# Group norm's pieces one engine a step, the end's fp8 rounding partly on GpSimd, and a later centring of the second chunk

## The chip, the cores and the metric

The kernel runs on one core of one Trainium2 chip. The metric is device time in microseconds: the median of several executions. A hardware profile of one more execution shows what each engine did. The engines are called PE (TensorE matmul; PEld is its weight load), DVE (VectorE), ACT (ScalarE), POOL (GpSimd) and SP (SyncE, which here only issues DMAs). Each works through its own queue in order; semaphores make one wait for another.

## The reference

The input x is 4 images of 64 x 64 positions with 96 channels, all in fp32. Cut to what matters:

```python
x = x + conv(_gn(x))            # _gn: group norm, 32 groups of 3 channels, over a whole image
t = tokens(x)                   # 4096 tokens of 96 channels per image
t = t + attn(_ln_t(t))          # 6 heads, no softmax: (q k^T) v, so k^T v comes first
t = t + ffn(_ln_t(t))           # 96 -> 384 -> 96, operands rounded to fp8 (e5m2), sums to fp16

# conv: layer norm, a projection to value, gate, delta and to A, B, C (16 states a channel)
h_new = d * (A_t * h) + d * (B_t * u_t)      # over the 4096 positions in turn
y = g_t * sum(C_t * h_new)                   # then a projection back to 96 channels

# ffn
h = relu(q_acc(q_acc(q_mul(x) @ q_mul(W1).T) + q_mul(b1)))
y = q_acc(q_acc(q_mul(h) @ q_mul(W2).T) + q_mul(b2))
```

The attention has no softmax, so its whole effect on an image is one 97 x 96 matrix, made from the Gram matrix of all tokens of the image. An image's attention can only start when its last token has been through the conv.

## The kernel before, in words

**Tiling.** An image is cut into 8 chunks of 512 tokens (NCH); 4 images give N = 32 chunks. The conv's state has 16 x 96 = 1536 rows, 12 tiles of 128 rows (NT). So the body has K = 384 steps: one step is one tile of one chunk, a 128 x 512 scan along time. In step s the loop at L1401 issues B's projection and copy for tile s+3 (L804, L811), A's for s+1 (L819, L823), C's for s (L844), POOL's multiply for s+2 (L814), the scan (L830), C's multiply (L854 on DVE, or L860 on ACT and L863 on POOL), and then `call(s)`, which runs what was put down for that step with `at(step, fn)`. The order of the work is thus written out by hand: the order in which a step issues its instructions is the order of each engine's queue.

**PSUM.** Matmul results go to banks by tag (L95): A 2, B 1, C 1, D 1 and M 3. All that is not a projection of the scan takes the M ring in turn; the fourth user of the ring waits until the first bank was read.

**Around the body.** For each chunk a `Front` (L659) centres and scales with the group norm's result (L670, L673), does the layer norm, splits the result into a high and a low part, and projects it. `tail` (L907) sums the states, projects, adds, normalizes (L396 on ACT, or L403 on DVE), adds to the Gram matrix and writes the transposed tokens to DRAM. `ffn` (L1059) fetches them (L1071), applies the attention matrix (a_ps, L1076), adds (L1081), takes layer-norm statistics on DVE (L371, L373), their root on POOL (L378, L392; with L383 and L384 if ACT is to normalize), normalizes to fp8, transposes (xq_ps, L1091), rounds (xq, L1098), and makes three 128 x 512 pieces of the hidden layer (h_ps, L1102).

**Group norm.** `group_norm` (L629) puts the pieces of images 1 to 3 into steps of the image before. Sums of all chunks are gathered by ACT (L574). Then L654 puts down six pieces: moments in step 1 after the last chunk's sum, mean in step 2, root in 4, diagonal in 6, spread and spread_out in 8. A piece holds instructions of several engines: moments has two on DVE (L581, L582) and three on POOL (L583 to L585); mean has a matmul (L590), two reads on DVE (L592, L594) and two on POOL (L596, L597); root has a matmul (L602), DVE (L604) and POOL (L605).

**Weights.** The weights of attention and ffn are transposed on PE and copied out on DVE in the same step (L334 to L359), one weight every 12 steps from step 20.

**The start and the end** are not in steps. They go through `Plan` (L412): jobs with an engine, a cost, what they follow, and the buffers they take and free. `run` lays them out greedily by cost, tries random changes of rank (`tries`, 800 for the end) and keeps the order with the earliest end by its own costs; the jobs are then issued in that order. Gaps that it expects on PE are filled with matmuls that nobody reads (`awake`, L1434). In the start the second chunk's centring on POOL follows a job `calm` at time 22 (L1257, L1328). There the weights of the projections are split: a high part on ACT (`high`, L301), a low part on DVE or POOL (`low`, L259), then copies by SP (L262, L263).

**The end** is what does not fit into the body: the last three chunks of image 2 and the ffn of all of image 3, whose attention matrix needs the last chunk. For each chunk: ACT copies three hidden pieces to fp16 (h, L1119), DVE adds the bias and takes relu (L1123), ACT rounds all three to fp8 at once (hq, L1127), PE projects (y_ps, L1133), the result is rounded to fp16 (DVE for odd chunks, L1141; ACT for even ones, L1143), and POOL adds bias (L1148) and x (L1155); DVE does it for the last two chunks. In image 3 DVE normalizes the even chunks (`vector`, L1067), ACT the odd ones. Chunks are written (image, chunk), such as (3,7).

Of the kernel before, what the change touches and what calls it, by code (L numbers as in the profile page):

```python
# [9 lines left out]
F32 = mybir.dt.float32  # L10
# [3 lines left out]
AF = mybir.ActivationFunctionType  # L14
# [14 lines left out]
NT = NCG * NSH  # L29
# [34 lines left out]
def conv_attn_hybrid_kernel(  # L64
# [38 lines left out]
    def bank(tag, shape, name):  # L103
        return psum.tile(shape, F32, tag=tag, name=name, bufs=BANKS[tag])
# [229 lines left out]
    def weights_attention():  # L334
        ps = bank("M", [C, CA], "wq_ps")
        nc.tensor.transpose(ps, w_qkv[:, 0:C], ident[:CA, :CA])
        nc.vector.tensor_copy(w_qt[0:C, :], ps)

    def weights_ffn1():
        ps = bank("M", [C, HID], "w1_ps")  # L340
        for m in range(NK):
            nc.tensor.transpose(ps[:, m * P : (m + 1) * P], w1_sb[:, m, :], ident)
        nc.vector.tensor_copy(w1_q, ps, saturate=False)

    def weights_ffn2():
        ps = bank("M", [P, NK, C], "w2_ps")
        for m in range(NK):
            nc.tensor.transpose(ps[:, m, :], w2_sb[:, m * P : (m + 1) * P], ident[:C, :C])
        nc.vector.tensor_copy(w2_q, ps, saturate=False)

    def weights_bias():
        ps = bank("M", [P, NK], "b1_ps")
        nc.tensor.transpose(ps, b1_sb, ident[:NK, :NK])
        b1_8 = small.tile([P, NK], F8, tag="b1_8", name="b1_8", bufs=1)
        nc.vector.tensor_copy(b1_8, ps, saturate=False)
        nc.vector.tensor_copy(b1_q, b1_8)
        b2_8 = small.tile([P, C], F8, tag="b2_8", name="b2_8", bufs=1)
        nc.vector.tensor_copy(b2_8, b2_sb, saturate=False)
        nc.vector.tensor_copy(b2_q, b2_8)  # L359
# [52 lines left out]
    class Plan:  # L412
# [10 lines left out]
        def job(self, engine, cost, fn, *args, after=(), take=(), free=(), late=0.0):  # L423

            j = dict(
                engine=engine, cost=cost, fn=fn, args=args, take=take, free=free, late=late,
                after=[a for a in after if a], tail=None, end=None, rank=self.rank,
            )
            self.jobs.append(j)
            return j  # L430
# [96 lines left out]
    def at(step, fn, *args):  # L527
        steps.setdefault(step, []).append((fn, args))
# [4 lines left out]
    class GroupNorm:  # L533
# [45 lines left out]
        def moments(self):  # L579
            t = small.tile([C, 2], F32, tag="gt", name=f"gt_{self.b}", bufs=2)  # L580
            nc.vector.tensor_reduce(t, self.s, AX.X, ALU.add)  # L581
            nc.vector.tensor_scalar_mul(t, t, 1.0 / L)  # L582
            nc.gpsimd.tensor_tensor(self.mv[:, 0:1], t[:, 0:1], self.c, ALU.subtract)  # L583
            nc.gpsimd.tensor_tensor(t[:, 0:1], t[:, 0:1], t[:, 0:1], ALU.mult)
            nc.gpsimd.tensor_tensor(self.mv[:, 1:2], t[:, 1:2], t[:, 0:1], ALU.subtract)  # L585


        def mean(self):
            ps = bank("M", [C, 2], f"gm_ps_{self.b}")
            nc.tensor.matmul(ps[:, 0:1], lhsT=third, rhs=self.mv[:, 0:1], start=True, stop=True)  # L590
            self.m = small.tile([C, 2], F32, tag="gm", name=f"gm_{self.b}", bufs=2)
            nc.vector.tensor_copy(self.m[:, 0:1], ps[:, 0:1])  # L592
            w = small.tile([C, 1], F32, tag="gw", name=f"gw_{self.b}", bufs=2)
            nc.vector.tensor_tensor(w, self.mv[:, 0:1], ps[:, 0:1], ALU.subtract)  # L594
            engine = nc.gpsimd if self.b else nc.vector
            engine.tensor_tensor(w, w, w, ALU.mult)  # L596
            engine.tensor_tensor(w, w, self.mv[:, 1:2], ALU.add)  # L597
            self.w = w

        def root(self):  # L600
            ps = bank("M", [C, 2], f"gv_ps_{self.b}")
            nc.tensor.matmul(ps[:, 0:1], lhsT=third, rhs=self.w, start=True, stop=True)  # L602
            v = small.tile([C, 1], F32, tag="gv", name=f"gv_{self.b}", bufs=2)
            nc.vector.tensor_scalar(v, ps[:, 0:1], 1e-5, None, ALU.add)  # L604
            nc.gpsimd.tensor_tensor(self.m[:, 1:2], v, mhalf[0:C, 0:1], ALU.pow)  # L605


        def diagonal(self, k0=0, k1=2):
# [20 lines left out]
    def group_norm(b, s0):  # L629
        q = {}  # L630

        def make():
            q["g"] = GroupNorm(b)
            q["g"].first()

        def call(name, *args):
            getattr(q["g"], name)(*args)

        when = [s0 + AT["sums"] + NT * n for n in range(NCH)]
        if b == 1:
            when = [8, 15, 22, 29, 36, 43, 50, 57]
        if b > 1:
            at(when[0] - 7, load_gx, b, 0)
        at(when[0] - 2, make)
        for n in range(NCH):
            if n:
                at(max(when[n] - 7, when[n - 1]), load_gx, b, n)
            at(when[n], call, "sums", n)  # L650
            at(when[n] + AT["sums_out"] - AT["sums"], call, "sums_out", n)
        for n, name in ((1, "moments"), (2, "mean"), (4, "root"), (6, "diagonal"), (8, "spread"),
                        (8, "spread_out")):
            at(when[-1] + n, call, name)  # L654


    split, rep, gate = {}, {}, {}
# [233 lines left out]
        {"ACT": 0.5, "DVE": 2.5, "POOL": 1.5},  # L891
    )
    end.last = {}
    end.tries = 800

    def place(plan, s0):

# [161 lines left out]
    def ffn(b, i, s0):  # L1059
# [4 lines left out]
        def tile_of(tag, drain_tag, shape, dtype, name):  # L1064
            return sb(drain_tag if phase["end"] else tag, shape, dtype, f"{name}_{nm}")

        vector = b == B - 1 and i % 2 == 0  # L1067

        def fetch():
            v["xa"] = next_of(xal_t, "xal")  # L1070
# [53 lines left out]

        def quant():
            v["hq"] = sb("bu", [P, NK, TC], F8, f"hq_{nm}")
            nc.scalar.activation(v["hq"], v["h16"], AF.Copy, saturate=False)  # L1127

        def project_out():
            ps = v["ps"] = bank("A" if phase["end"] else "M", [P, J, C], f"y2_ps_{nm}")  # L1130
# [6 lines left out]

        def round_out():
            v["y16"] = tile_of("y16", "xs", [P, J, C], F16, "y16")
            if phase["end"] and i % 2:  # L1140
                nc.vector.tensor_copy(v["y16"], v["ps"])  # L1141
            else:
                nc.scalar.copy(v["y16"], v["ps"])  # L1143

        def bias_out():
            last_two = phase["end"] and b == B - 1 and i > NCH - 3
# [23 lines left out]
        )  # L1170
        done = place(plan, s0)
        if fetch not in done and b < B - 1:
            at(K - 4, fetch)
            done.add(fetch)
        if store in done:
            return
# [10 lines left out]
        def job(engine, cost, fn, *args, **kw):  # L1187
            return None if fn in done else end.job(engine, cost, fn, *args, **kw)
# [10 lines left out]
        if hidden not in done:  # L1199
            r, h, c = [], None, None  # L1200
            for m in range(NK):
                h = job("PE", 0.24, hidden, m, after=[a, h], take=[f"M:{m}{nm}"],
                        free=[f"h:{nm}"] if m == 2 else [])
                c = job("ACT", 0.57, round_hidden, m, after=[h, c],
                        take=[f"rep:{nm}"] if m == 0 else [], free=[f"M:{m}{nm}"])
                r.append(job("DVE", 0.5, relu_vector, m, after=[c]))
            a = job("ACT", 1.5, quant, after=r, take=[f"bu:q{nm}"], free=[f"rep:{nm}"])
        a = job("PE", 0.5, project_out, after=[a], take=[f"A:y{nm}"], free=[f"bu:q{nm}"])
        a = job(*(("ACT", 0.48) if vector else ("DVE", 0.56)), round_out, after=[a],
                take=[f"xs:{nm}"], free=[f"A:y{nm}"])  # L1210
        last_two = b == B - 1 and i > NCH - 3
        a = job(*(("DVE", 0.6) if last_two else ("POOL", 0.95)), bias_out, after=[a], take=[f"xl:{nm}"], free=[f"xs:{nm}"])
# [9 lines left out]
    def planned_start():  # L1222
# [20 lines left out]
        b = mm(0.8, bias_turn, after=[b], key="M:b")  # L1243
        b = job("DVE", 0.35, bias_out, after=[b], free=["M:b"])
        a = job("DVE", 0.4, q.aggregate, after=a)
        m = job("DVE", 1.1, q.mean, after=[a])
        r = job("DVE", 0.7, q.root, after=[m], late=0.9)
        g = []
        for n, a in enumerate((m, r)):
            a = job("ACT", 0.37, q.diagonal, n, n + 1, after=[a, *g])  # L1250
# [9 lines left out]
        wd = job("SP", 1.0, split_copies, w_dug[:, 0], w_dug[:, 1], w_dug[:, 2], after=[ld], late=2.2)  # L1260
        wr = [job("ACT", 0.45, repeat, n, k, after=[(hd, ld)[n]]) for n in range(2) for k in range(2)]
        w = {"rep": job("SP", 1.0, split_copies, *(w_rep[:, n] for n in range(3)), after=wr, late=2.2)}
        for sh in range(NSH):
            plan.rank = 3 * sh - 3
            for k in range(3):
                t = job("ACT", 0.83, high, k, sh, after=[raw[k]])
                if sh < 2:
                    t = job("DVE", 0.8, low, k, sh, nc.vector, after=[t])
                else:
                    plan.rank = 1 if k == 0 else 3 * sh - 3  # L1270
                    t = job("POOL", 1.3, low, k, sh, nc.gpsimd, after=[t, calm])
                    low_b = t if k == 0 else low_b
                v = w_bac[k][:, :, :, sh * P : (sh + 1) * P]
                w[k, sh] = job("SP", 1.0, split_copies, *(v[:, n] for n in range(3)), after=[t], late=2.4)
        plan.rank = -4
# [49 lines left out]


        plan.rank = 1
        a = job("POOL", 1.0, second.centre, nc.gpsimd, after=[*g, calm])  # L1328
        a = job("POOL", 1.0, second.scale, nc.gpsimd, after=[a])
        a = job("DVE", 1.1, second.stats, after=[a])  # L1330
        a = job("POOL", 1.8, second.ln.rstd, after=[a])
# [35 lines left out]

    second = planned_start()

    for n, fn in enumerate((weights_attention, weights_ffn1, weights_ffn2, weights_bias)):  # L1370
        at(NT + 8 + NT * n, fn)
    for b in range(B):
        for i in range(NCH):
            g = b * NCH + i
# [96 lines left out]
```

## Time and profile before

| what | us |
|---|---|
| median of 3 executions | 1183.2 |
| their range | 1182.86 to 1183.66 |
| the profiled execution, its own time | 1184.49 |
| its span, first to last instruction | 1182.8 |
| PE busy (of the span) | 1140.1 (96%) |
| PEld busy | 874.6 (74%) |
| DVE busy | 1113.2 (94%) |
| ACT busy | 817.3 (69%) |
| POOL busy | 1030.3 (87%) |
| mean granted PE clock | 0.988 of full |

The shares are means over three stages with different limits: a start of about 60 us, the body, and an end from about 1105 us on. So the stages are to be read apart: busy time by stretch, who waited for whom in a stretch, and the chain that ended last. A row of instructions gives engine, line, operation, output and inputs, shape and count, then the busy time and the mean duration of one. Matmuls overlap, so a full PE row says that PE always had something in flight. The granted clock is the share of the full PE clock that the core was given; fillers such as `awake` count as busy.

### The profile page before, as it was taken

What the parts mean: (1) busy time and instruction counts of PE and PEld (TensorE: products, weight loads), DVE (VectorE), ACT (ScalarE), POOL (GpSimd) and SP (SyncE); (2) the same over time, 40 slices, a digit from 0 to 9 for tenths busy, and PEclk for the clock granted to TensorE, in tenths of its full rate; (3) what the DMA queues carried; (4) which work ended last, traced back from release to release, by engine and by line L of the source; (5) the groups of instructions that cost most, each with busy time, mean ns of one, the idle gap of its engine ahead of it and who ended that gap; (6) DMA issues with size and microseconds to landing.
All of it is one profiled execution on the core that took longest, in us unless ns stands there. A gap on an engine that the chain in (4) does not pass through costs nothing. (4 is left out here: it accounts for less than half of the span.)

```text
span 1182.8 us, 19203 instructions
## 1 busy us (share of the span) xinstructions
PE 1140.1 (96%) x5899; PEld 874.6 (74%) x5899; DVE 1113.2 (94%) x2093; ACT 817.3 (69%) x1826; POOL 1030.3 (87%) x1176
## 2 busy tenths in 40 slices
PE   5999999999999999999999999999999999999885
PEld 4777777677777777777777777777777777777573
DVE  6999999899999999999999999999999999999865
ACT  4666655556556777877877777777776777776476
POOL 5798887788889899999999999999999999988554
PEclk8999999899999999999999999999999999999989
DMA  7676776687776776787777777766777778667221
GB/s 185 142 167 143 167 155 154 141 176 161 170 160 151 161 162 157 158 190 170 161 159 161 172 162 166 171 158 152 159 165 169 160 162 185 147 145 153 60 75 47
DMA packets 104288, 182.12 MB, mean 154 GB/s; under 512 B 42637, under 2 KB 50769, under 8 KB 104186
## 3 DMA queue, kind: packets, MB, share of 16 engines
q1 hardware_dynamic: 90060, 106.96, 37.3%
q0 software_dynamic: 13536, 73.93, 31.4%
q8 instruction: 46, 0.75, 0.3%
q14 instruction: 56, 0.46, 0.1%
q10 hardware_dynamic: 590, 0.02, 0.0%
HBM read 69.12 MB, written 24.77 MB: 79 GB/s over the span
## 5 line engine op out<-in xcount | busy, mean ns | idle before, releaser
L814 POOL TENSOR_TENSOR bu<-bu,rep 128x512 f32<-128x512 f32 x384 | 512.9, 1345 | 43.3 <-ACT state L840 34.8
L830 DVE TENSOR_TENSOR_SCAN h<-Aps,state,bu 128x512 f32<-128x512 f32 x336 | 426.2, 1268 | 0.7 <-POOL ch L863 0.5
L811 ACT ACTIVATE bu<-Bps,b_bac 128x512 f32<-128x512 f32 x384 | 263.1, 685 | 198.5 <-PE Bps L269 192.9
L823 DVE SCALAR_TENSOR_TENSOR Aps<-Aps,b_bac,rep 128x512 f32<-128x512 f32 x384 | 281.9, 734 | 8.2 <-PE Aps L269 8.2
L269 PE MATMUL Bps<-xs,w 128*128 128x512 f32 x768 | 268.0, 430 | 7.7 <-ACT bu L811 7.1
L269 PE MATMUL Aps<-xs,w 128*128 128x512 f32 x768 | 242.2, 396 | 1.2 <-DVE h L830 1.0
L863 POOL TENSOR_TENSOR ch<-ch,h 128x512 f32<-128x512 f32 x126 | 170.4, 1352 | 7.9 <-ACT ch L860 3.7
L269 PEld LDWEIGHTS Aps<-xs,w 128*128 128x128 f32 x768 | 143.9, 188 | 37.3 <-DVE h L830 3.0
L269 PEld LDWEIGHTS Bps<-xs,w 128*128 128x128 f32 x768 | 126.7, 191 | 51.2 <-ACT bu L811 15.4
L269 PE MATMUL Aps<-xl,w 128*128 128x512 f32 x384 | 152.0, 396 | 0.0
L269 PE MATMUL Bps<-xl,w 128*128 128x512 f32 x384 | 151.7, 395 | 0.0
L269 PE MATMUL Dps<-xs,w 128*128 128x512 f32 x384 | 121.0, 396 | 0.0
L269 PE MATMUL Cps<-xs,w 128*128 128x512 f32 x384 | 120.6, 395 | 0.0
L854 DVE SCALAR_TENSOR_TENSOR ch<-Dps,b_bac,h 128x512 f32<-128x512 f32 x160 | 118.6, 742 | 0.9 <-PE Dps L269 0.5
L869 POOL DMA_DIRECT2D ch<-ch x94 | 89.6, 953 | 0.3 <-DMA ch<-ch 0.3
L269 PEld LDWEIGHTS Bps<-xl,w 128*128 128x128 f32 x384 | 72.5, 189 | 17.7
L269 PEld LDWEIGHTS Dps<-xs,w 128*128 128x128 f32 x384 | 72.3, 188 | 17.7
L269 PEld LDWEIGHTS Aps<-xl,w 128*128 128x128 f32 x384 | 72.2, 188 | 17.7
L269 PEld LDWEIGHTS Cps<-xs,w 128*128 128x128 f32 x384 | 72.0, 188 | 17.6
L860 ACT ACTIVATE ch<-Cps,b_bac 128x512 f32<-128x512 f32 x94 | 64.6, 688 | 24.1 <-PE Cps L269 24.1
L269 PE MATMUL Dps<-xl,w 128*128 128x512 f32 x192 | 75.9, 395 | 0.0
L269 PE MATMUL Cps<-xl,w 128*128 128x512 f32 x192 | 75.8, 395 | 0.0
(200 smaller groups left out, 2045.2 us busy)
## 6 DMA issues: line engine op xcount, KB each, us to landing
ch<-ch POOLq DMA_DIRECT2D x94, 768.0 KB, 6.7
rep<-ddd SPq DMA_DIRECT2D x124, 384.0 KB, 7.4
ddd<-dd SPq DMA_DIRECT2D x31, 384.0 KB, 3.2
xl<-lo SPq DMA_DIRECT2D x62, 128.0 KB, 2.5
x<-in_x_dram SPq DMA_DIRECT2D x32, 192.0 KB, 3.0
xatd<-xat SPq DMA_DIRECT2D x32, 192.0 KB, 3.6
xal<-xatd SPq DMA_DIRECT2D x32, 192.0 KB, 2.8
out_dram<-o SPq DMA_DIRECT2D x32, 192.0 KB, 2.1
```

The source lines that it names most:

```text
L269: nc.tensor.matmul(ps, lhsT=wt[:, n], rhs=mv, start=(n == 0), stop=(n == 2))
L811: nc.scalar.activation(self.bu, self.b_ps, AF.Identity, bias=self.bias(0))
L814: nc.gpsimd.tensor_tensor(self.bu, self.bu, rep[self.b, self.i][:, 1, self.cg], ALU.mult)
L823: nc.vector.scalar_tensor_tensor(self.a_ps, self.a_ps, self.bias(1), rep[self.b, self.i][:, 0, self.cg], ALU.add, ALU.mult,)
L830: nc.vector.tensor_tensor_scan(self.h, self.a_ps, self.bu, 0.0 if self.i == 0 else state[self.sh, self.cg], ALU.mult, ALU.add,)
L854: nc.vector.scalar_tensor_tensor(self.slot(), self.c_ps, self.bias(2), self.h, ALU.add, ALU.mult)
L860: nc.scalar.activation(self.ch, self.c_ps, AF.Identity, bias=self.bias(2))
L863: nc.gpsimd.tensor_tensor(self.ch, self.ch, self.h, ALU.mult)
L869: nc.gpsimd.dma_start(chs[g, 0], chs.pop((g, sh)), accum_op=ALU.add)
```

## The change

Four edits, and two that follow them:

- **Group norm.** The six pieces become eleven, each of one engine, one to a step, from the step after the last chunk's sums: moments (DVE), variances (POOL), a matmul, mean (DVE), squares (POOL), a matmul, offset (DVE), root (POOL), diagonal (ACT), spread (PE), spread_out (ACT). In the start the pieces are called together in the old order.
- **Weights.** A weight's copy on DVE is put one step after its transposes on PE.
- **The end.** A chunk whose number is divisible by 3 is rounded to fp8 on ACT, the others on POOL. All of y is rounded to fp16 on ACT. In image 3 only chunks 0 and 4 are normalized by DVE; 2 and 6 go to ACT. The plan's costs follow, relu's cost goes from 0.5 to 0.47, and 1500 orders are tried instead of 800. The order of the chunks changes with it: (2,6) before (2,7), and in image 3 chunk 0 goes from third place to last but one.
- **The start.** The second chunk's centring follows POOL's first low split instead of `calm`.
- **Fetches.** Those of image 2 that are left are put into step K - 1 instead of K - 4.

```diff
     def weights_attention():
         ps = bank("M", [C, CA], "wq_ps")
         nc.tensor.transpose(ps, w_qkv[:, 0:C], ident[:CA, :CA])
-        nc.vector.tensor_copy(w_qt[0:C, :], ps)
+        return lambda: nc.vector.tensor_copy(w_qt[0:C, :], ps)
...
+        def variances(self):
+            t = self.t
             nc.gpsimd.tensor_tensor(self.mv[:, 0:1], t[:, 0:1], self.c, ALU.subtract)
...
+        def group_sums(self, name):
+            self.ps = bank("M", [C, 2], f"g{name}_ps_{self.b}")
+            nc.tensor.matmul(
+                self.ps[:, 0:1], lhsT=third, rhs=self.mv[:, 0:1] if name == "m" else self.w,
+                start=True, stop=True,
+            )
...
-        for n, name in ((1, "moments"), (2, "mean"), (4, "root"), (6, "diagonal"), (8, "spread"),
-                        (8, "spread_out")):
-            at(when[-1] + n, call, name)
+        chain = (
+            ("moments",), ("variances",), ("group_sums", "m"), ("mean",), ("squares",),
+            ("group_sums", "v"), ("offset",), ("root",), ("diagonal",), ("spread",), ("spread_out",),
+        )
+        for n, args in enumerate(chain):
+            at(when[-1] + AT["sums_out"] - AT["sums"] + 1 + n, call, *args)
...
-    end.tries = 800
+    end.tries = 1500
...
-        vector = b == B - 1 and i % 2 == 0
+        vector = b == B - 1 and i % 4 == 0
...
-            nc.scalar.activation(v["hq"], v["h16"], AF.Copy, saturate=False)
+            if i % 3 == 0:
+                nc.scalar.activation(v["hq"], v["h16"], AF.Copy, saturate=False)
+            else:
+                nc.gpsimd.tensor_copy(v["hq"], v["h16"], saturate=False)
...
-            if phase["end"] and i % 2:
-                nc.vector.tensor_copy(v["y16"], v["ps"])
-            else:
-                nc.scalar.copy(v["y16"], v["ps"])
+            nc.scalar.copy(v["y16"], v["ps"])
...
-            at(K - 4, fetch)
+            at(K - 1, fetch)
...
-                r.append(job("DVE", 0.5, relu_vector, m, after=[c]))
-            a = job("ACT", 1.5, quant, after=r, take=[f"bu:q{nm}"], free=[f"rep:{nm}"])
+                r.append(job("DVE", 0.47, relu_vector, m, after=[c]))
+            a = job(*(("ACT", 1.5) if i % 3 == 0 else ("POOL", 1.6)), quant, after=r, take=[f"bu:q{nm}"], free=[f"rep:{nm}"])
...
-        a = job("POOL", 1.0, second.centre, nc.gpsimd, after=[*g, calm])
+        a = job("POOL", 1.0, second.centre, nc.gpsimd, after=[*g, first_low])
...
+    def turned(step, fn):
+        at(step + 1, fn())
+
     for n, fn in enumerate((weights_attention, weights_ffn1, weights_ffn2, weights_bias)):
-        at(NT + 8 + NT * n, fn)
+        at(NT + 8 + NT * n, turned, NT + 8 + NT * n, fn)
```

The lines of the changed kernel lie up to 27 further down: POOL's new rounding is L1152, ACT's L1150, h L1141, relu L1145, and y L1165.

## The prediction

> **What bounds the kernel now.** I read the busy time by stretches first, then the chain that ended last, then each queue of the end. Columns of the stretches: length, then busy time (x instructions) of PE, PEld, DVE, ACT, POOL, then granted clock, DMA share, GB/s.
>
> ```profile
> 600.00:800.00 200.00, 199.35 (x1052) 153.84 (x1051) 194.49 (x364) 153.84 (x354) 188.28 (x218) 1.00 0.73 164
> 1109.20:1142.00 32.80, 31.06 (x202) 22.67 (x201) 21.44 (x94) 18.50 (x34) 15.37 (x26) 0.84 0.25 74
> 1142.00:1174.10 32.10, 23.52 (x198) 16.08 (x195) 21.39 (x75) 30.67 (x52) 17.09 (x24) 1.00 0.18 50
> ```
>
> In the body PE and DVE are both full; POOL has 6% left and ACT a quarter. From 1142 to 1174 ACT is the bound (30.67 of 32.10) while POOL is half idle. Before 1142 no engine but PE is full, and PE runs part of it at half clock:
>
> ```profile
> 1126.00:1128.00 2.00, 2.00 (x13) 2.00 (x13) 0.81 (x2) 1.68 (x2) 0.10 (x1) 0.59 0.36 98
> 1132.00:1134.00 2.00, 2.00 (x12) 2.00 (x11) 1.51 (x4) 2.00 (x6) 1.82 (x4) 0.50 0.03 8
> 1136.00:1138.00 2.00, 2.00 (x15) 1.34 (x14) 0.04 (x1) 0.59 (x1) 0.86 (x1) 0.85 0.73 201
> ```
>
> The chain that ended last says the same of the last 35 us: start, length, engine and line.
>
> ```profile
> 1168.54 2.40 ACT h L1119 x5
> 1170.94 2.76 ACT hq L1127 x2
> 1173.71 0.05 issue
> 1173.75 0.70 PE y_ps L1133 x12
> 1174.45 0.02 issue
> 1174.48 0.57 DVE y L1141
> 1175.05 0.02 issue
> 1175.07 0.57 DVE yb L1148
> 1175.64 0.02 issue
> 1175.66 1.15 DVE o L1155
> ```
>
> So the pace of the end is ACT's: copies (0.48 each), quantizations (1.38), then a tail of 5.9 us. DVE ends at 1176.8; 6.0 us follow to the end of the span, and 1.7 lie around it (1184.5 against 1182.8).
>
> **Part 1, group norm and weight copies in pieces.** Nothing is added or removed; per image eleven pieces stand one to a step, so no engine meets in one step a piece it must wait for. In the chain of the three later images DVE waits for none of its small reads. What waits is POOL: L583 for DVE's sums 4.0 us in 3 times, L605 1.1 us in two (of 6.7, 5.6 is the start's). POOL's idle time costs nothing while the scans are fed, and DVE's scans stand end to end there (728.43, 731.50, 734.25, 736.79). PE's sequencer waits before the first sum, half a microsecond in each of three images:
>
> ```profile
> L590 PEldq EVENT_SEMAPHORE  x4: 51/503/649, 12.2 to 726.4; - x4
> ```
>
> Bounds: a gain of 3 x 0.6 = 1.8 if PE's wait is all on the path; a loss where an "M" bank (three in all) is now held a step longer. That is so ten times (four weights, six sums). Only behind the biases is the third user of the ring so close that it must wait: L931's transposes began at 193.24, and the delayed copy would free the bank near 193.7, a loss of 0.5. As PE shows 0.65 us idle in 200, I take a third of the gain, -0.6, and keep -1.8 and +0.5.
>
> **Part 2, the start.** POOL's first low split (1.16: the two at 23.18 take 2.31) goes before centre and scale (1.03 and 1.08). All end where they ended, at 25.5; centring comes 1.16 later, near 24.4. DVE's queue reads it at 30.46 (L371), so 6 us cover it; without that cover it would cost 1.2. SP's copies of that split are issued at 28.1, after others, so nothing is gained. ACT's two copies for the third weight move one or two places forward: one (0.84) falls into ACT's wait of 0.72 before 30.95. Bounds -0.3 to +0.3, by the waits of these rows; I take 0. The later fetches of image 2 (K - 1 instead of K - 4) keep their places in SP's queue and change only which of (2,6) and (2,7) comes first; that is in part 3.
>
> **Part 3, the end.** By engine, from the rows of the end:
>
> - ACT: 7 quantizations leave (chunks 5, 7 of image 2; 1, 2, 4, 5, 7 of image 3), -7 x 1.38 = -9.7; 6 roundings of y come from DVE, +6 x 0.37 = +2.2; chunks 2 and 6 are normalized on ACT, +2 x 1.44 = +2.9. Net -4.6.
> - DVE: -6 x 0.56 - 2 x 1.0 = -5.4.
> - POOL: +2 x 0.6 for two shifts (L383, L384), +7 quantizations.
>
> A quantization on POOL (128x1536, f16 to fp8) isn't in the trace. Nearest rows:
>
> ```profile
> L208 POOL CAST ident<-ident 128x128 fp8e5<-128x128 f32 x1 | 0.3, 291 | 0.1
> L220 POOL MEMSET xn<- 128x512 fp8e5 x2 | 1.1, 528 | 0.1
> L1148 POOL TENSOR_TENSOR yb<-y,b_q 128x384 f16<-128x384 f16 x30 | 27.7, 923 | 7.7 <-ACT y L1143 5.9 <-DVE y L1141 1.6
> ```
>
> Memsets of 1 and 512 columns take 0.10 and 0.53: 0.84 ns a column. At that pace the cast's 0.291 holds 0.18 of fixed cost, and 1536 columns give 0.18 + 1.29 = 1.5; with the 0.19 of a one-column L584 it is 1.4. If the fixed cost were only a memset's 0.10, a column would cost 1.5 ns and the piece 2.4. The two-input row's 2.4 ns a column would need less than no fixed cost, so I drop it. I take 1.5, by the cast row, and keep 1.4 and 2.4.
>
> I then walked the changed queues with these durations. (1) Image 3's attention matrix: a_ps of chunk (2,6) goes first, so the output of (3,7) starts 1.05 earlier; its root comes at 1118.6 instead of 1120.2, and rmat near 1124.2 instead of 1125.4: -1.2. (2) That gain is lost: PE's h_ps of (2,7) is now split by the a_ps of (3,6) and (3,1). At half clock, from 1124.2: two a_ps 3.0, xq 0.4, a filler 0.5, y 1.0, two h 0.8, two a_ps 3.4, the third h 0.5: 1133.8. ACT's copy of it stands ahead of the normalizing of (3,3): copy 0.5, two normalizings 2.9, three small pieces 1.3, and 0.6 for PE between them, so the copies of (3,3) start at 1139.1 (before: 1138.45). (3) From there ACT has 24 copies (11.5), 4 normalizings (5.8), 2 quantizations (2.8), 6 xq (2.9) and 6 y (2.2), 25.1 us, to the last h copy of (3,7), which would end at 1164.2. (4) POOL takes the quantization of (2,7) at 1134.9, as soon as that third copy is through relu. Behind it in its queue stand four roots with shifts (1.97 each), two without (1.4), four more quantizations (1.57 with the gap) and eleven pieces of bias and total (0.97): 29.3 us without a gap, to 1164. ACT waits for them: 1.75 before (3,5)'s normalizing, 1.1 and 0.9 at (3,0) and (3,6), 1.25 in four small ones, 5.0 in all. The last h copy ends near 1169.2 (before 1170.9). (5) The tail: relu 0.3, POOL 1.5, PE 0.75, ACT 0.45, DVE 0.6 and 1.3, and six hops of 0.06: 5.3 (before 5.9). DVE ends near 1174.5 instead of 1176.8: **-2.3**. POOL is late next.
>
> The new POOL pieces meet DVE's:
>
> ```profile
> 1140.35 1.03 DVE L403 TENSOR_SCALAR xn<-x,mv_f,rstd_f 128x96 fp8e5<-128x96 f32 x4
> 1161.93 2.93 DVE L403 TENSOR_SCALAR xn<-x,mv_f,rstd_f 128x96 fp8e5<-128x96 f32 x4
> ```
>
> The second ran while POOL was busy without a gap (1160.9 to 1168.3) and took 1.9 more; I counted this once, at (3,0). [...]
>
> **Sum.** -2.3 - 0.6 + 0 = -2.9: the profiled execution's 1184.5 becomes 1181.6. The median shown is 1.3 below that execution, so I forecast 1183.2 - 2.9 = 1180.3.
>
> **Rivals.** (B) The half clock does not come back. It set in after PE's thin stretch from 1119 to 1126; the changed order has as many small matmuls there, so I expect it again, but one filler batch shrinks from three to one. Without it the third h_ps of (2,7) comes 3.3 earlier and POOL's run with it: end -5.6, time 1177.0. [...] (C) The gain is not there: POOL's order holds ACT longer than walked, since every root now queues behind quantizations; 2.9 more waits give 1183. For it: POOL has no gap for 29 us. (D) Slower: the piece costs 2.4 on POOL. Five pieces in the gapless run and the last in the tail, 6 x 0.9 = 5.4: end +3.1, with part 1 at nothing, 1186.3. It turns from 1.9 us a piece on (2.3 / 6 = 0.4 over 1.5). For it: the cast row allows it; against: memset's slope.
>
> **How the numbers follow.** A 45%, B 22%, C 18%, D 15%. A measurement of this kernel can tell about 0.2%, 2.4 us: under 1180.8 is faster, over 1185.6 slower. A's own range is 1178 to 1182.5; a fifth of it is no change. Faster 0.36 + 0.22 = 0.58, same 0.09 + 0.18 = 0.27, slower 0.15. The range reaches from below B (a further 1.2 of part 1) to D: 1175.8 to 1186.3.
>
> **What would show it.** L1152 on POOL 1.4 to 1.7 us; ACT under 27 us busy after 1142 with waits for POOL's nmr and for y_ps; POOL over 85% busy from 1135 to 1164; granted clock 0.5 for some 10 us near 1126; DVE's last piece near 1174.5; scans of the body end to end around L581 to L620. I am wrong if POOL's piece is near 2 us or more, if the clock stays at 1.0, or if the body moves by more than 2 us.

## The result and the profile after

| kernel | median, us | range | executions | ratio to before, 95% interval |
|---|---|---|---|---|
| before | 1183.03 | 1181.96 to 1183.66 | 4 | |
| changed | 1182.64 | 1180.44 to 1183.65 | 4 | 0.9995 (0.9978 to 1.0012) |

No change that the measurement can tell. The forecast was 1180.3, the range 1175.8 to 1186.3. The profiled executions differ more: 1184.49 before, 1182.40 after (spans 1182.8 and 1180.7).

A sum near zero can hide large terms, so I read the trace by stages first. The body's 384 scans are its milestones: they are the same instructions in both kernels. Worked out from the starts of the scans in the two traces:

| stage | before, us | changed, us | difference |
|---|---|---|---|
| to the first scan (start) | 34.7 | 35.9 | +1.2 |
| first scan to last (body) | 1073.6 | 1068.6 | -5.0 |
| ... of this, scans 60 to 72 | 37.7 | 33.3 | -4.4 |
| last scan to the end (end) | 74.4 | 76.1 | +1.7 |

None of the three is what I had written (0, -0.6, -2.3). In the start and the end, windows of half clock lie differently in the two executions (before 13.6 to 20.4 and 1126.3 to 1136.6 us; changed 12.0 to 22.3, 29.1 to 32.5 and four, 17.1 us together, between 1117.9 and 1158.9), so their differences are not yet the change's.

The stretches after, moved 3.8 us forward as the last scan was (length, busy time of PE, PEld, DVE, ACT, POOL, granted clock, DMA share, GB/s):

```profile
600.00:800.00 200.00, 200.00 (x1053) 154.01 (x1052) 195.03 (x370) 153.53 (x354) 188.23 (x216) 1.00 0.75 167
1105.40:1138.20 32.80, 28.79 (x196) 21.69 (x194) 21.22 (x95) 18.50 (x39) 18.71 (x30) 0.85 0.25 68
1138.20:1170.30 32.10, 23.57 (x164) 15.16 (x163) 23.84 (x61) 25.97 (x53) 23.65 (x32) 0.89 0.19 56
```

ACT went from 30.67 to 25.97 of 32.10 in the last stretch, and POOL from 17.09 to 23.65: the work moved as planned. But the clock is 0.89 where it was 1.00, and now no engine is full. The chain that ended last, its final pieces:

```profile
1167.73 2.25 DVE h L1145 x6
...
1170.10 1.47 POOL hq L1152
...
1171.62 0.70 PE y_ps L1158 x12
...
1172.40 0.49 ACT y L1165
...
1173.58 1.15 DVE o L1177
```

POOL's rounding and the wait of PE's sequencer, by their lines (durations shortest, median, longest, in ns):

```profile
L1152 POOL CAST hq<-h x7: 1462/1465/1560, 1115.4 to 1170.1; 128x1536 fp8e5<-128x1536 f16 x7
...
L597 PEldq EVENT_SEMAPHORE  x5: 51/51/51, 11.9 to 729.6; - x5
```

The rounding costs 1.47 us; I had taken 1.5. The half microseconds in which PE's sequencer waited for the group norm (503 and 649 ns before) are gone.

### The profile page after: what moved, and what is told of

Its sections match the earlier page's. It is cut to its first block, busy times and chain, and to the rows that moved or that the text cites. A ratio compares the mean times of both kernels' runs of the same rounds, so it can differ in the third digit from the quotient of the medians.

```text
span 1180.7 us, 19182 instructions
## 1 busy us (share of the span) xinstructions
PE 1139.8 (97%) x5882; PEld 874.3 (74%) x5882; DVE 1114.0 (94%) x2079; ACT 813.6 (69%) x1833; POOL 1040.7 (88%) x1187
## 3 DMA queue, kind: packets, MB, share of 16 engines
q1 hardware_dynamic: 90060, 106.96, 37.7%
```

## The experiments

Each kernel was profiled once and timed against the kernel before on the same chip. Different rows come from different chips, so the ratios are to be compared before the medians. The stages of each profile, in us:

| kernel | median, us | ratio to before, 95% | first scan | scans 60-72 | last scan to end |
|---|---|---|---|---|---|
| before, first profile | 1183.03 | | 34.7 | 37.7 | 74.4 |
| changed | 1182.64 | 0.9995 (0.9978-1.0012) | 35.9 | 33.3 | 76.1 |
| 1 before again | 1183.19 | 1.0001 (0.9990-1.0012) | 35.9 | 36.4 | 74.7 |
| 2 part 1 alone | 1180.29 | 0.9973 (0.9962-0.9983) | 35.1 | 33.3 | 74.4 |
| 3 part 3 alone | 1187.56 | 1.0031 (1.0019-1.0043) | 35.9 | 36.4 | 78.2 |
| 4 parts 1 and 2 | 1178.83 | 0.9963 (0.9951-0.9976) | 34.7 | 33.3 | 73.2 |
| 5 diagonal later | 1182.46 | 0.9992 (0.9979-1.0006) | 36.7 | 35.9 | 74.4 |
| 6 filler in the wait | 1182.34 | 0.9985 (0.9973-0.9998) | 36.2 | 34.8 | 73.6 |
| 7 tiny rounding | 1175.09 | 0.9922 (0.9903-0.9942) | 35.8 | 33.3 | 70.4 |
| 8 denser fillers | 1180.03 | 0.9970 (0.9960-0.9980) | 35.4 | 33.3 | 75.7 |
| 9 other form | 1182.67 | 0.9995 (0.9983-1.0006) | 36.2 | 33.3 | 77.2 |
| 10 rounding in three | 1180.43 | 0.9982 (0.9970-0.9994) | 35.8 | 33.3 | 75.0 |
| 11 fillers and form | 1178.20 | 0.9956 (0.9941-0.9972) | 34.3 | 33.3 | 74.3 |
| 12 POOL held back | 1176.79 | 0.9939 (0.9925-0.9952) | 34.2 | 33.3 | 72.5 |

### 1 to 4: the change in its parts

**Theory:** part 1 gained what the body gained, part 2 is nothing, and the end's change costs. **Rivals:** the half clock near 215 us belonged to one execution; the end's pieces are worth the 2.3 us and the clock fell badly once. Kernel 1 is the kernel before, unchanged.

> The kernel before, unchanged, profiled a second time. In the first profile PE waited 2.56 us for ACT's copy at 213 us, the granted clock was 0.5 from 215.0 to 221.8, and the scans numbered 60 to 72 took 37.7 us; in the changed kernel they took 33.3. Theory (the half clock belongs to the wait): half clock again between 212 and 222, 36 to 38 us for these scans. Rival (the half clock was chance of one execution): the wait of 2.5 us is there, the clock stays at 1.0, and the scans take some 34.5 to 35.5. For the start and the end: if the windows of half clock lie elsewhere than in the first profile (13.6 to 20.4 and 1126.3 to 1136.6), differences of 1 to 2 us in these stages are chance.

Kernel 2 has the diff's hunks of group norm and weights alone, kernel 3 those of the end and of the fetches, kernel 4 all but those of kernel 3.

> Only the group norm's pieces and the weights' copies are changed; start and end are as before. Theory: all of the gain seen in the body is part 1's, 4.4 us at the one place near 213 us and 0.5 to 0.7 in each of the two later images: 5.0 to 5.6 us in all, 1177.5 to 1178, ratio 0.9955. Rival (the place near 213 us is chance): 1.2 us, 1181.8, ratio 0.999. My prediction had 0.6 for it.

> Only the end is changed, with the later fetches. From the last scan to the end of the span it took 74.4 us before and 76.1 in the changed kernel. Theory (the end's change itself costs): 76 here too, 1.5 to 2 us slower, 1184.7, ratio 1.0014. Rival (the end's pieces are worth the 2.3 us that I predicted, and the clock's windows fell badly in one execution): 72 to 74, ratio 0.998.

> The changed kernel with the end of the kernel before. Theory (part 1 gains, part 2 is nothing, the end's change costs): the same as part 1 alone within 0.5 us, 1177.5 to 1178, ratio 0.9955, and 4 to 4.5 us faster than the changed kernel. Rival (the later centring costs the 1.2 us by which the first scan came late in the changed kernel): 1.2 us slower than part 1 alone, 1179, first scan near 36 us instead of 34.7.

**Measured.** Part 1 alone gains 3.2 us by its ratio (0.0027 x 1183), between theory and rival. Some of the distance to the theory is the first profile itself, whose half clock near 215 us lasted longer than in the later ones (below). With part 2 it is 4.4 (0.0037), and the two intervals overlap, so that part 2's share is not told from zero. Part 3 alone loses 3.7. The sum of kernels 3 and 4, -0.7, is the changed kernel's -0.6. So the change consists of a gain of some 4 us and a loss of some 4.

*The place near 215 us.* Kernel 1 shows it again. Timelines of PE and ACT in the first profile of before (start, length, instruction, in brackets the idle time before it and what ended it):

```profile
212.07 1.54 ACT L396 ACTIVATE z<-z,nmr_c,rstd_c 128x96 f32<-128x96 f32 x4 [1.53 <-POOL nmr_c L384]
213.51 0.63 ACT L612 ACTIVATE gdg<-ident,gm 96x96 f32<-96x96 f32 x2
214.05 0.58 ACT L564 ACTIVATE gc_ps<-gc_ps 96x512 f32<-96x512 f32 x1
...
214.88 0.67 ACT L811 ACTIVATE bu<-Bps,b_bac 128x512 f32<-128x512 f32 x1
...
215.61 1.22 PE L269 MATMUL Bps<-xs,w 128*128 128x512 f32 x2 [2.56 <-ACT bu L811]
```

In step 63 ACT's queue held, in a row, the normalizing of the next front chunk (late by 1.53, behind POOL, whose queue held the group norm's root, L605, ahead of that chunk's), the group norm's diagonal of image 1, and the first sum of image 2. ACT's copy of B stood behind all three; B has one bank, so PE waited 2.56 us. That wait is not the whole price. Stretches of the same profile:

```profile
212.00:216.00 4.00, 1.44 (x6) 0.91 (x5) 3.47 (x4) 3.54 (x11) 4.00 (x5) 0.87 1.01 227
216.00:220.00 4.00, 4.00 (x11) 3.13 (x11) 1.06 (x3) 0.77 (x2) 2.57 (x3) 0.50 0.70 185
```

and of part 1 alone (kernel 2):

```profile
216.00:220.00 4.00, 4.00 (x24) 2.74 (x22) 3.79 (x7) 2.20 (x7) 3.75 (x4) 1.00 0.84 194
```

The idle PE lost its clock: it is at 0.5 from 215.0 us on, before the wait is over. PE then does 11 matmuls in 4 us instead of 24, and DVE, which lives on them, is busy 1.06 of 4. The half clock lasted 6.8 us in the first profile and 3.4 in kernels 1 and 3; scans 60 to 72 took 37.7, 36.4 and 36.4. With part 1 they took 33.3 in all nine kernels that have it. The weights' copies, the other half of part 1, show nothing: scans 0 to 60, where all four lie, took 166.2 and 166.6 us in the two profiles of before, and 166.1 to 166.7 in eight of the nine kernels with part 1 (167.9 in kernel 9).

*The start.* The first scan comes at 35.4 to 36.7 us in nine of the fourteen profiles, the second one of the unchanged kernel among them, and at 34.2 to 35.1 in the other five. The granted clock (seventh number) tells why. Before, first profile:

```profile
30.00:34.00 4.00, 4.00 (x19) 3.20 (x18) 3.30 (x12) 2.62 (x5) 2.25 (x5) 1.00 0.63 127
```

Before, second profile (kernel 1):

```profile
30.00:34.00 4.00, 4.00 (x12) 3.16 (x11) 2.08 (x10) 2.03 (x4) 2.30 (x5) 0.58 0.53 104
```

The same kernel had full clock there once and half clock once, and its first scan came at 34.7 and 35.9. All nine late profiles have a stretch of half clock between 29.1 and 34.2 us, and none of the other five has. Kernel 4 has the later centring and full clock there, and its first scan comes at 34.7, as in the first profile of before:

```profile
30.00:34.00 4.00, 4.00 (x19) 3.26 (x18) 3.32 (x12) 3.35 (x6) 2.31 (x5) 1.00 0.64 128
```

So the changed kernel's +1.2 is a window of the clock and not the centring.

*The end.* 78.2 with part 3 alone and 76.1 in the changed kernel, against 73.2 to 74.7 in kernels 1, 2 and 4, which have the old end: the theory holds, and more strongly than I expected. The clock has a share in it. Before the last 10 us of its end, kernel 3 ran 23.9 us at half clock, against 3.4 to 17.1 in the four profiles of the old end. And the new order carries fewer fillers: 39 `awake` matmuls behind the last scan instead of 56.

### 5 and 6: one piece, and the clock by itself

Kernel 5 moves one piece of the kernel before:

```diff
-        for n, name in ((1, "moments"), (2, "mean"), (4, "root"), (6, "diagonal"), (8, "spread"),
+        for n, name in ((1, "moments"), (2, "mean"), (4, "root"), (7, "diagonal"), (8, "spread"),
```

> The kernel before, with one piece moved: the diagonal of the group norm (0.63 us of ACT) stands one step later, in step 64 + image offset instead of 63. Theory: in step 63 ACT has the normalizing, the diagonal and the next image's first sums in a row, so its copy of B is late, PE waits 2.56 us, and the wait takes the clock to 0.5. With 0.6 us less PE waits about 1.9; if that is too short for the clock to fall, scans 60 to 72 take 34 to 34.5 instead of 36.4 to 37.7, and the kernel gains 2 to 3.5 us. Rival (the gain needs all eleven pieces, or the waits of POOL and DVE behind the root): no more than 0.6 us gained, half clock still there.

Kernel 6 leaves every wait as it was and gives PE something to do in it:

```diff
+    def fill_wait():
+        ps = bank("M", [P, TC], "fill_wait")
+        for _ in range(10):
+            nc.tensor.matmul(
+                ps, lhsT=w_dug[:, 0, 0:P], rhs=w_bac[0][:, 0, 0], start=True, stop=True
+            )
+
+    at(64, fill_wait)
```

> The kernel before, with ten matmuls that nobody reads (128x512, about 0.235 us each) put into PE's queue at the end of step 64, where PE waits 2.56 us for ACT. The wait for ACT is not changed; only PE is not idle in it. Theory (the fallen clock is the larger part of the loss): no half clock near 215 to 222, scans 60 to 72 take 34.5 to 35.3 instead of 36.4 to 37.7, a gain of 1.5 to 2.5 us. Rival (the wait itself is the loss): scans as before, 36.4 or more.

**Measured.** Kernel 5: PE's wait fell from 2.56 to 2.05 us, the clock still fell to 0.5 for 3.4 us, and scans 60 to 72 took 35.9. That is the rival: one piece less in the row isn't enough. Which of the other pieces is needed was not tried. Kernel 6: the clock stays up (1.00 from 212 to 224 us), and the scans take 34.8:

```profile
217.45 0.73 PE L269 MATMUL Bps<-xs,w 128*128 128x512 f32 x2 [0.26 <-ACT bu L811]
```

ACT's copy is as late as it was, but PE was idle for 0.26 us only. So of the 3.1 to 4.4 us that the place cost over 33.3, the wait itself is 1.5 (34.8 - 33.3), and the clock that it took away 1.6 to 2.9. In the times this shows as 0.9985 (0.9973 to 0.9998).

### 7 and 8: the loss in the end, POOL's or the clock's

Kernel 7 is the changed kernel in its own order with nearly free roundings on POOL: it leaves out nearly all of the rounding of seven chunks.

```diff
-                nc.gpsimd.tensor_copy(v["hq"], v["h16"], saturate=False)
+                v["hq"] = hq_zero
+                nc.gpsimd.tensor_copy(hq_zero[:, 0, 0:1], v["h16"][:, 0, 0:1], saturate=False)
```

> The changed kernel in the same order, but POOL's seven roundings cast one column instead of 1536 (some 0.2 us instead of 1.47), and PE multiplies a tile of zeros for these seven chunks: the rounding of seven of the 9 + 2 last chunks is left out. Theory (the end's loss is POOL's: its time in the queue and DVE pieces stretched beside it, 4.8 us on normalizing and 2.2 more on relu): from the last scan to the end 69 to 72 us instead of 76 to 78, DVE's normalizing of an end chunk 1.0 to 1.5 us instead of 2.8 and 4.1. Rival (the order and the clock are at fault): 74.5 to 76.

Kernel 8 puts nearly twice as many fillers into the end's gaps on PE:

```diff
-                    for _ in range(int(max(0.0, t - self.time.get(e, t) - 0.4) / 0.4)):
+                    for _ in range(int(max(0.0, t - self.time.get(e, t) - 0.4) / self.pace)):
...
+    end.pace = 0.24
```

> The changed kernel in the same order, with 75 fillers on PE in the end instead of 39 (one for each 0.24 us of expected gap instead of one for 0.4). Theory (POOL and DVE set the end's loss): windows of half clock go from 17 us to under 7 before the last 10 us, but the end changes by less than 1.5 us: 74.5 to 77. Rival (the clock sets it): 72 to 74, the kernel 2.5 to 4 us faster. If fillers delay PE's real work: 77 to 79.

**Measured.** Kernel 7: 70.4 instead of 76.1, as the theory had it; half clock before the last 10 us fell from 17.1 us to 10.2 as well, so the gain is not the queue's and the waits' alone. One part of the theory missed: DVE's normalizing of (3,0) still took 2.88, beside POOL's other work. Kernel 8: half clock before the last 10 us fell from 17.1 us to 6.8; in its profile the end is only 0.5 shorter, but the median of ten executions is 1180.03 against 1182.64. The mean clock of these ten is 0.990 to 0.992, of the changed kernel's four 0.983 to 0.985. So here both have a share: with POOL's rounding free the end gains 5.7 us in the profile and the kernel 8.6 by the ratios, with the clock held up 0.5 and 3.0. My pair of theories was too simple.

How POOL's roundings reach the end is seen in two queues side by side. DVE and POOL of the changed kernel:

```profile
1115.40 1.47 POOL L1152 CAST hq<-h 128x1536 fp8e5<-128x1536 f16 x1
...
1157.46 0.93 POOL L1170 TENSOR_TENSOR yb<-y,b_q 128x384 f16<-128x384 f16 x1
1158.33 1.46 POOL L1152 CAST hq<-h 128x1536 fp8e5<-128x1536 f16 x1
...
1115.47 2.17 DVE L406 TENSOR_SCALAR xa<-x,mv_a,rstd_a 128x96 f32<-128x96 f32 x4 [1.24 <-POOL rstd_a L395]
...
1157.53 4.08 DVE L406 TENSOR_SCALAR xn<-x,mv_f,rstd_f 128x96 fp8e5<-128x96 f32 x4 [0.98 <-POOL rstd_f L395]
```

and of kernel 7:

```profile
1115.40 0.19 POOL L1153 CAST hq_zero<-h 128x1 fp8e5<-128x1 f16 x1
...
1115.47 1.05 DVE L406 TENSOR_SCALAR xa<-x,mv_a,rstd_a 128x96 f32<-128x96 f32 x4 [1.24 <-POOL rstd_a L395]
```

The same four pieces at the same moment take 2.17 us beside the cast of 1.47 and 1.05 beside one of 0.19. At 1157.5 POOL has instructions without a gap, each of DVE's four pieces waits, and 1.05 becomes 4.08. Taken over the whole end, DVE's instructions lasted 12.2 us longer than the shortest of their kind in the changed kernel, 7.8 before and 7.0 in kernel 7.

### 9 and 10: what DVE waits for

Kernel 9 writes DVE's normalizing in another form, hoping that it does not wait for POOL:

```diff
-                nc.vector.tensor_scalar(
-                    dst[:, j, 0:C], src[:, j, :], self.mv[:, j, 0:1], self.r[:, j : j + 1],
-                    ALU.subtract, ALU.mult, **kw,
+                nc.vector.scalar_tensor_tensor(
+                    dst[:, j, 0:C], src[:, j, :], self.mv[:, j, 0:1],
+                    self.r[:, j : j + 1].to_broadcast([P, C]), ALU.subtract, ALU.mult, **kw,
```

> The changed kernel in the same order; DVE's normalizing (z of the first chunk, the last xa, xn of two chunks of the end) is written as scalar_tensor_tensor instead of tensor_scalar, with the root as a second input. In the body's rows the three-input form keeps its 0.74 us beside a busy POOL. Theory (a tensor_scalar on DVE waits for POOL's whole instructions, the three-input form doesn't): normalizing of a chunk 1.0 to 1.5 us in the start and the end, where tensor_scalar took 3.3, 2.2, 2.8 and 4.1; the first scan 1 to 2 us earlier at the same clock, the end 2.5 to 4 us shorter (72 to 73.5). Rival (POOL slows every form alike, or what is late in the end is POOL's queue): pieces of 2 us and more, the end 75 to 77.

Kernel 10 cuts POOL's instruction:

```diff
-                nc.gpsimd.tensor_copy(v["hq"], v["h16"], saturate=False)
+                for m in range(NK):
+                    nc.gpsimd.tensor_copy(v["hq"][:, m, :], v["h16"][:, m, :], saturate=False)
```

> The changed kernel in the same order; each of POOL's seven roundings is three casts of 512 columns instead of one of 1536. By the measured 1.47 us and the 0.18 of fixed cost that I had worked out, three take 1.8. Theory (DVE's pieces wait for whole POOL instructions): a DVE piece then waits 0.6 instead of 1.47 for a cast, its stretch in the end falls from 7 us on normalizing and relu to some 5, POOL has 2.5 us more: end 75 to 77. Rival (DVE is slowed by a share of the time, not by whole instructions): stretch 7 or more, end 77 to 78.

**Measured.** Kernel 9 refutes its theory: the three-input form takes 3.40 us in the start (3.29 in the changed kernel) and 2.19 for xa (2.17), and the time is the changed kernel's.

```profile
21.35 3.40 DVE L406 SCALAR_TENSOR_TENSOR z<-z,mv_c,rstd_c 128x96 f32<-128x96 f32 x4 [0.17 <-POOL rstd_c L395]
```

The body's 0.74 us, from which I had argued, is a form with one input in PSUM; the new one has both in SBUF. Whether that is what sets them apart, no run shows. Kernel 10 is nearer to its theory than to its rival. The end, 75.0, is at the lower edge of the theory's 75 to 77; the stretch on normalizing and relu, counted as before, is 6.0 us (theory some 5, rival 7 or more):

```profile
1115.21 1.73 POOL L1153 CAST hq<-h 128x512 fp8e5<-128x512 f16 x3
...
1115.28 1.95 DVE L406 TENSOR_SCALAR xa<-x,mv_a,rstd_a 128x96 f32<-128x96 f32 x4 [1.24 <-POOL rstd_a L395]
```

Three casts take 1.73. The four pieces of xa by their durations (shortest, median, longest, in ns), changed kernel and kernel 10:

```profile
L406 DVE TENSOR_SCALAR xa<-x,mv_a,rstd_a x4: 319/322/1453, 1115.5 to 1117.3; 128x96 f32<-128x96 f32 x4
L406 DVE TENSOR_SCALAR xa<-x,mv_a,rstd_a x4: 319/618/640, 1115.3 to 1116.9; 128x96 f32<-128x96 f32 x4
```

The longest was 1.45 us beside the cast of 1.47; beside casts of 0.6 the longest is 0.64. In the changed kernel that piece ends 0.06 us behind the cast (1116.93 and 1116.87); in kernel 10 each of the three long pieces ends 0.06 us behind one of the three casts. These long pieces thus waited for the POOL instruction under way to end, not for a share of the time. Although POOL has more work, DVE's instructions lose 11.0 instead of 12.2, the end takes 75.0 instead of 76.1, and the median is 1180.43 instead of 1182.64; the two intervals of the ratios overlap.

### 11 and 12: a version that beats both

Kernel 11 is kernel 4 with the fillers of kernel 8 and the form of kernel 9.

> Parts 1 and 2 with the end of before, the denser fillers in the end (0.24 us of expected gap for one) and the three-input form of DVE's normalizing. If the gains are separate: 1178.8 for parts 1 and 2, 1 to 2 less by the form in the start, 1 to 2 less by the form at the end's 2.9 us piece, 1 to 2 less by the fillers: 1174 to 1176, ratio 0.993. Rival (the fillers only helped where POOL left PE thin, and the start is set by another wait): 1178 to 1179.

Kernel 12 is kernel 4 with the fillers alone, and a copy of one number on POOL that waits for DVE's normalizing of the first chunk:

```diff
+        def hold():
+            t = small.tile([P, 1], F32, tag="hold", name="hold", bufs=1)
+            nc.gpsimd.tensor_copy(t, first.t[:, J - 1, 0:1])
+
+        h = job("POOL", 0.2, hold, after=[a])
+        for t in pool_lows:
+            t["after"].append(h)
```

> Parts 1 and 2, the end of before with the denser fillers, and one wait added in the start: a copy of one number holds POOL's first low split, and all behind it, until DVE has normalized the first chunk. So DVE's normalizing meets no POOL instruction. Theory (each of DVE's four pieces waits for a whole POOL instruction): normalizing takes 1.1 to 1.4 us instead of 3.3, and as POOL has slack until 31 us, the first scan comes 1.5 to 2 us earlier than in the kernels with full clock there (32.5 to 33.2 against 34.3 and 34.7): about 1176.5, ratio 0.9945. Rival (the start then waits for the splits that DVE makes beside POOL, or for the copies of the weights): normalizing 1.1 to 1.4, but the first scan at 34 to 34.7, 1178 to 1178.8.

**Measured.** Kernel 11: the rival, 1178.2; both additions together are 0.6 us below kernel 4, within the intervals. Kernel 12: the fastest of those that do the whole work, 1176.79 us, ratio 0.9939 (0.9925 to 0.9952), its five executions within 0.8 us of each other at a mean clock of 0.991 to 0.994. That is the time of the theory, but not by its way: in the start the rival is right.

```profile
20.93 1.05 DVE L406 TENSOR_SCALAR z<-z,mv_c,rstd_c 128x96 f32<-128x96 f32 x4 [0.18 <-POOL rstd_c L395]
...
26.71 3.36 DVE L259 TENSOR_TENSOR w<-raw,w 128x384 fp32r<-128x384 f32 x2
...
22.04 1.38 POOL L1313 COPY hold<-z 128x1 f32<-128x1 f32 x1 [1.15 <-DMA w_rep<-w_rep]
```

The normalizing takes 1.05 instead of 3.3, but DVE's splits behind it meet POOL in its place (3.36 for two; 1.59 before), and POOL's copy of one number waits for DVE in turn (1.38). The first scan is at 34.2, no earlier than in kernel 11. That kernel 12 is 1.4 us faster than kernel 11 is not explained by this. In its profile the clock is full from 22.8 us to the last 5, and the end is 1.8 us shorter; whether holding POOL back brings that about, or where the clock's windows fell, five executions do not tell; the intervals of the two ratios overlap.

## Why the prediction was right in its sum and wrong in its steps

The time lies in the range, 2.3 us from the forecast and within what the measurement can tell of no change. It got there by two errors of opposite sign, and that is luck; of the outcomes, "faster" had been given 58% and "same", which came, 27%.

- **"What bounds the kernel now".** Borne out for the last stretch: ACT was full there and is no longer (25.97 of 32.10 us).
- **Part 1, "-0.6", bounds -1.8 to +0.5: failed.** By kernel 2 it is a gain of 3.2 us (2.0 to 4.5 by the interval of its ratio, beyond the bound of 1.8). The half microseconds at PE's sequencer are right as far as they go: scans 72 to 383, images 2 and 3 among them, took 869.8 before and 868.5 to 868.8 with part 1. The step that failed is "DVE's scans stand end to end there": I read it off one image's chain (728 to 737 us) and let it stand for all three. In image 1's, at 212 to 222 us, PE waited 2.56 us and lost its clock. "POOL's idle time costs nothing" looked past the way it went: through POOL's root to ACT's normalizing, to ACT's copy of B, to PE. The page before had it in the row of the clock, eighth digit, and I followed that row only into the end:

```profile
PEclk8999999899999999999999999999999999999989
```

- **Part 2, "0": not contradicted.** The centring had its 6 us of cover; POOL waited for the second chunk's statistics until 31.58 in both kernels (L378 before, L381 after). The start's +1.2 us is the clock.
- **Part 3, "-2.3": failed, also in its sign.** By kernel 3 it is +3.7. The mis-sized term is not the rounding (1.5 forecast, 1.47 measured), nor POOL's queue (forecast full over 29 us; 25.40 of 29.00 busy), nor the tail behind the last h copy (5.3 forecast; 5.5 from 1169.2 to 1174.7). Counted from the last scan, the matrix of image 3 (rmat) was forecast to be done at 15.8 us and was at 19.0 (before: 17.0); from there to the end of the last h copy I had 45.0 and it took 45.6. So 3.2 of the 4.0 us that the walk is off lie ahead of rmat. (1) DVE's xa, whose gram matrix rmat needs, waited 1.1 us for the rounding of (2,6), which the new order put right beside it; kernel 7, without that wait and with full clock there, has rmat at 16.3. (2) PE ran at half clock from 1117.9 to 1121.3; in kernel 8, with full clock there and xa still waiting, rmat is at 17.4. So 1.1 are xa's wait, 1.6 the clock, and 0.5 (15.8 to 16.3) I can't place. I had let no window of half clock fall before rmat. That the stretch behind rmat fits (45.0 and 45.6) is luck: I had ACT wait 5.0 us there for POOL's roots, and it waited for none of them, but 8.0 us for PE's y_ps and xq_ps. The rows of rmat before and changed, the changed kernel's half clock ahead of it, and what its ACT waited for most between 1118 and 1165 us (in total, times, longest):

```profile
1125.18 0.25 DVE L1037 COPY rmat<-r_ps 97x96 f32<-97x96 f32 x1
```

```profile
1123.35 0.24 DVE L1059 COPY rmat<-r_ps 97x96 f32<-97x96 f32 x1
```

```profile
1117.90:1121.30 3.40, 3.40 (x23) 2.73 (x23) 2.00 (x12) 1.71 (x4) 1.59 (x4) 0.50 0.19 57
```

```profile
ACT y L1165 <- PE y_ps L1158: 4.0, 4, 1.5
ACT xq L1120 <- PE xq_ps L1113: 4.0, 3, 1.8
ACT xat L957 <- PE xat_ps L953: 3.3, 1, 3.3
ACT h L1141 <- PE h_ps L1124: 1.6, 2, 1.0
ACT h L1141 <- POOL hq L1152: 0.8, 1, 0.8
```

- **"I counted this once, at (3,0)": the term of DVE's waits.** It came three times (xa 1.1, (3,4) 1.8, (3,0) 3.0), 5.9 us in place of 1.9; only xa's 1.1 is shown to be on the path. In the sum of the walk even the 1.9 has no row of its own. The walk used this wait as a remark and not as a row: each such piece of DVE beside a busy POOL should have been charged with the POOL instruction under way (in xa 1.45 us for a piece of 0.32, beside the cast of 1.47).
- **Rivals.** B (the half clock does not come back) did not come in this profile: 17 us in four windows instead of 10 in one. That is no mark of the change alone, as the second profile of before has 17 us in three windows. C (the gain is given back) is what the total shows, 1182.64 against 1183, but for another reason: DVE's waits and the clock, not ACT behind POOL's roots. D needed a piece of 1.9 us or more and falls.
- **What would show it.** "I am wrong if the body moves by more than 2 us": it moved by 5.0.

At a nearly equal clock a loss is left: kernels 8, 11 and 12 all have the denser fillers and mean clocks of 0.989 to 0.995, and by their ratios kernel 8, with the new end, is 1.7 us behind kernel 11 (the intervals overlap) and 3.7 behind kernel 12 (they do not, but kernel 12 also holds POOL back in the start). What stays open is how this loss divides between POOL's longer queue and DVE's waits. Kernel 7 removes both. Kernel 10 shortens the waits, lengthens the queue, and gains 1.1 in the profile and 1.5 by the ratios, whose intervals overlap; it leans to the waits and does not show it. A form of DVE's normalizing with one input outside SBUF was not tried, nor the changed end with smaller roundings and denser fillers together.

## What to carry to other kernels

Price an idle PE with the clock that it loses as well: look in the page for every digit of the clock's row that is below 9, find the wait ahead of it, and count its half-clock microseconds into what an edit at that place can win or lose (here a wait of 2.56 us with 6.8 us at half clock behind it). Before work is moved to POOL, charge those DVE pieces that will run beside it and that the traces show waiting for it with the wait for a whole POOL instruction: here the `tensor_scalar` of normalizing (a piece of xa 1.45 us instead of 0.32), its form with two inputs in SBUF (3.40 for four pieces) and the splits (3.36 for two instead of 1.59). Cut the POOL instruction if the DVE piece is on the path (the longest piece of xa then took 0.64). When two profiles differ by a microsecond or two, line up common milestones stage by stage and profile the kernel before a second time: here 1.2 us in the start moved with the clock's windows and not with the edit.

## What the runs showed of the hardware

- Ahead of the one at the end, the half clock came in stretches of 3.41, 6.83 and 10.24 us, in different places in different executions of one kernel (13.6 to 20.4 in one profile of before; 12.9 to 19.7 and 29.9 to 33.4 in the other). In the clock's record of each of the 14 profiles, all starts and ends of half clock up to the last start lie on one grid of 3.413 us, to 2 ns (in the first profile of before, 13.61, 20.43, 214.99, 221.82, 1126.35, 1136.59 and 1177.55 us); where it lies differs from execution to execution. I counted PE's idle time in each step of that grid at full clock, between the first stretch of half clock and the last. All 27 steps with 1.7 us or more of idle were followed by half clock, and none with less than 0.86; from 0.86 to 1.7, 28 of 161 were. In the first profile of before, half clock followed on 1.95 us of idle (the step from 211.58) and on 0.87 (from 1122.94), and not on 1.48 (from 20.43). So idle time alone does not settle it. The wait near 215 us left 1.95 to 2.58 us of idle in the step ahead.
- The kernel before varied from 1180.25 to 1185.82 us in 19 executions on one chip; the six under 1182.8 had a mean clock of 0.987 to 0.993, the seven over 1184.2 one of 0.983 to 0.987. So its spread goes with how much of the time is at half clock.
- The wait between DVE and POOL goes both ways: in kernel 12 POOL's copy of one number took 1.38 us behind DVE's splits; kernel 7's cast of one column took 0.19.
